# A two-layer graph network on one core: the first step's adjacency product of two pairs as one two-level product, and gate weights kept inside a matrix that has become free

## The chip, the core and the metric

The kernel runs on one core of a Trainium2 chip. The metric is device time in microseconds, lower is better. A run of the kernel before takes 1511.48 us (median of three, 1511.04 to 1511.8). Engines: PE (matmul) with its weight loads PEld, DVE (vector), ACT (activations), POOL (GpSimd), and SP, whose queue issues every DMA here. Everything is float32.

## What is computed

`x` is 32 batches of 512 nodes by 128 channels; `adj` is one 512 x 512 matrix, the same for all.

```python
# layer 0, K = 3, both adjacency matrices are adj
x_all = [x, adj x, adj^2 x, adj^3 x, adj x, adj^2 x, adj^3 x]
x = layernorm(x + einsum('bnik,iok->bno', x_all, weight_1))
# layer 1, five steps from h = x
m_in = m_out = adj @ h
av = concat(m_in, m_out)
u3 = h @ u3_w.T + u3_b
z  = sigmoid(av @ w3_w.T + w3_b + u3)
r  = sigmoid(av @ w4_w.T + w4_b + u3)
hv = tanh(av @ w5_w.T + w5_b + (r * h) @ u5_w.T + u5_b)
h  = (1 - z) * h + z * hv
# after the steps
x = layernorm(x + h)
```

Since `m_in` and `m_out` are equal, the two halves of w3, w4 and w5 are added once, to 128 x 128 matrices.

## The kernel before

**Work.** Batches go in 16 pairs. Each pair passes layer 0 (`layer0`), then five steps (`pair`, the loop over `s`), then the residual and the norm. A step of a pair is: the product adj h of both batches, a product with u3 for each batch, and `gates` for each batch (products with w4, w3, w5 of m, with u5 of r h; sigmoids and a tanh on ACT; sums on DVE; the update of h on POOL, L925). Then h is turned from channels-by-nodes to nodes-by-channels for the next step's product, by a DVE transpose in blocks of 32 and two DMA legs through DRAM (`turn`: four puts and a fetch), or, for the last steps of pairs 14 and 15 (`ON_PE`), by PE transposes.

**Products in seven terms.** A 2 x 2 block product is made from seven block products instead of eight, with sums of blocks formed beforehand. `seven` holds the pattern: seven PE terms into three PSUM banks, where four results are copied out by ACT and three added by DVE. `pair_product` uses it on one level for two batches: seven terms of two matmuls of 256 columns (128 columns each of left operand), with four POOL sums of 128 x 256 in front. The sums of adj's blocks lie in `T`. `quad_product` uses it on two levels for four batches: an upper product of seven, each of which is again a product of seven quarter blocks. Four of the upper terms run together (the A half, left sums in `SA`, results in `PA`), then three (the B half, `SB`, results in `M`), and five DVE sums join them (L672). The second-level sums of adj's blocks lie in `TT`. It is 49 matmuls of 128 columns. Before the change, `quad_product` serves layer 0 from pair 2 on, with pairs 2 and 3, 4 and 5, and so on; the steps use `pair_product`.

**Order.** Nothing is ordered by the hardware's own luck: `Plan` is a list scheduler that runs when the kernel is built. Each operation has an engine, a length, its predecessors, the buffers that it takes and gives back, and a key. Whenever an engine is free, it gets the ready operation with the lowest key whose buffers are free. The order in which operations come out is each engine's instruction order on the chip. Keys come from `KEYS` (one start per pair), plus 30 and `LONG` = 19 per step. Buffers are counted in `slots`: eight PSUM banks, so many tiles of each name, and two counts without memory, `two` (products in the making) and `inside` (pairs between entry and end). The sums that form `TT` are planned right after `T`; the summed gate weights w3s, w4s, w5s have tiles of their own.

**h0.** The input of layer 1 is kept for the residual. Except for the last three pairs it is written to DRAM after step 0's product has read it (hd<-h), and fetched back for the end.

**Gates.** `mm(dst, w, src, first, last)` is one matmul with 512 moving columns: the weights are stationary, m (128 channels x 512 nodes) moves.

Of the kernel before, what the change touches and what calls it, by code (L numbers as in the profile page):

```python
# [9 lines left out]
F32 = mybir.dt.float32  # L10
AF = mybir.ActivationFunctionType
ALU = mybir.AluOpType
PSUM = bass.MemoryType.PSUM

P = 128
NK = 4
N = NK * P
H = NK // 2
HN = N // 2
R = 32  # L20
NR = P // R
STEPS = 5
ON_PE = {14: 2, 15: 2}
KEYS = [8.0, 22.0, 60.0, 88.0, 108.0, 144.0, 174.0, 188.0, 210.0, 244.0, 274.0, 310.0, 338.0, 368.0, 384.0, 396.0]
LONG = 19.0
KEPT = 3
FIRST = 2
SINGLE = 2
EPS = 1e-5
# [95 lines left out]
def gnn_resnorm_kernel(  # L125
# [17 lines left out]
    nc = tc.nc  # L143
    NP = x.shape[0] // 2

    const = ctx.enter_context(tc.tile_pool(name="const", bufs=1))
    work = ctx.enter_context(tc.tile_pool(name="work", bufs=1))
    small = ctx.enter_context(tc.tile_pool(name="small", bufs=16))
    psum = ctx.enter_context(tc.tile_pool(name="psum", bufs=1, space=PSUM))
    dram = ctx.enter_context(tc.tile_pool(name="dram", bufs=1, space=bass.MemoryType.DRAM))  # L150

    def tiles(tag, n, shape=(P, N), pool=work):
        return [pool.tile(list(shape), F32, tag=f"{tag}_{i}", name=f"{tag}_{i}") for i in range(n)]

    slots = dict(
        bank=tiles("bank", 8, pool=psum),
        d=tiles("d", 6, (NR, R, NR, P), dram),
        hd=tiles("hd", 6, (P, 2, NK, P), dram),
        xg=tiles("xg", 2, (P, 2, NK, P)),
        xT=tiles("xT", 3),  # L160
        M=tiles("M", 1, (P, 4, N)),
        SA=tiles("SA", 1, (P, 25, P)),
        SB=tiles("SB", 1, (P, 15, P)),
        UY=tiles("UY", 2, (P, 4, N)),
        h0=tiles("h0", 4, (P, 2, NK, P)),
        hT=tiles("hT", 8),
        X=tiles("X", 3),
        uT=tiles("uT", 6),
        rh=tiles("rh", 2),
        z=tiles("z", 3),  # L170
        m=tiles("m", 5),
        S=tiles("S", 2, (P, 7, H, P)),
        v=tiles("v", 4),
        two=[None] * 3,
        inside=[None] * 14,
    )
    plan = Plan(slots)
# [12 lines left out]
    T = const.tile([P, 4, H, HN], F32, tag="T", name="T")  # L190
    TT = const.tile([P, 7, 4, P], F32, tag="TT", name="TT")
    make_identity(nc, ident)
# [35 lines left out]

    TT_sums = []
    for i, n, of in (  # L230
        (0, 4, lambda k, c: T[:, :, k, c]),
        (4, 2, lambda k, c: at.rearrange("p (o k) c -> p o k c", o=2)[:, :, k, c]),
        (6, 1, lambda k, c: at[:, H + k : H + k + 1, HN + c.start : HN + c.stop]),
    ):
        lo, hi = slice(0, P), slice(P, HN)
        b11, b12, b21, b22 = of(0, lo), of(0, hi), of(1, lo), of(1, hi)
        t = lambda j, i=i, n=n: TT[:, i : i + n, j, :]

        def emit(b11=b11, b12=b12, b21=b21, b22=b22, t=t):
            for j, (a, b) in enumerate(((b12, b11), (b22, t(0)), (b22, b12), (b21, t(1)))):  # L240
                nc.vector.tensor_tensor(t(j), a, b, ALU.subtract)  # L241

        TT_sums.append(plan("DVE", (2.8, 1.7, 1.12)[i // 3] if i else 2.8, emit, after=T_sums, key=22.0))

# [13 lines left out]
    w0_ready = plan("DVE", 2.3, layer0_weights, after=[w0_in], give=[("UY", "w0")], key=-40.0)  # L260


    ready = []

    def gate_weight(src, name):
        halves = lambda: plan[name][:, : 2 * P].rearrange("p (h o) -> p h o", h=2)
        w = const.tile([P, P], F32, tag=name, name=name)
        emit = lambda: nc.sync.dma_start(halves(), src.rearrange("(h c) o -> c h o", c=P))
        got = plan("SP", 0.45, emit, take=[("z", name)], key=-60.0, late=6.5)
        emit = lambda: nc.vector.tensor_tensor(w, halves()[:, 0, :], halves()[:, 1, :], ALU.add)  # L270
        ready.append(plan("DVE", 0.28, emit, after=[got], give=[("z", name)], key=-30.0))
        return w

    def plain(src, name):
        t = const.tile(list(src.shape), F32, tag=name, name=name)
        ready.append(plan("SP", 0.45, lambda: nc.sync.dma_start(t, src), key=-55.0, late=5.0))
        return t

    w3s, w4s, w5s = (gate_weight(s, n) for s, n in ((w3, "w3s"), (w4, "w4s"), (w5, "w5s")))
    u3s, u5s = plain(u3, "u3s"), plain(u5, "u5s")  # L280
    b3s, b4s, b5s = plain(b3, "b3s"), plain(b4, "b4s"), plain(b5, "b5s")
    ub3s, ub5s = plain(ub3, "ub3s"), plain(ub5, "ub5s")
    hv_b = const.tile([P, 1], F32, tag="hv_b", name="hv_b")
    hv_ready = plan("DVE", 0.1, lambda: nc.vector.tensor_tensor(hv_b, b5s, ub5s, ALU.add), after=ready, key=-30.0)
    weights = ready + [hv_ready]

# [131 lines left out]
    an_of = lambda km: plan[f"an{km // H}"].rearrange("p b k c -> p (b k c)").rearrange("p (k n) -> p k n", k=H)  # L418
    an_ready = []
    for km in range(NK):  # L420
        emit = lambda km=km: transposes(plan[f"ba{km}"], lambda k: at[:, k, chunk(km)])
        take = [("bank", f"ba{km}")] + ([("h0", f"an{km // H}")] if km % H == 0 else [])
        tr = plan("PE", 0.44, emit, after=at_in, take=take, key=20.0)
        emit = lambda km=km: nc.scalar.copy(an_of(km)[:, km % H], plan[f"ba{km}"])
        an_ready.append(plan("ACT", 0.59, emit, after=[tr], give=[("bank", f"ba{km}")], key=20.0))
# [49 lines left out]
    for i, (a, b, op) in enumerate(  # L475
        (
            (A21, A22, ALU.add),
            (at2S[:, 0], A11, ALU.subtract),
            (A11, A21, ALU.subtract),
            (A12, at2S[:, 1], ALU.subtract),  # L480
        )
    ):
        emit = lambda i=i, a=a, b=b, op=op: nc.vector.tensor_tensor(at2S[:, i], a, b, op)
        A2_sums.append(plan("DVE", 0.69, emit, after=squared + A2_sums[-2:], key=21.0))

    half_bank = lambda bank: bank[:, :HN]
# [65 lines left out]
    def quad_product(X_of, name, after, key):  # L552
# [48 lines left out]
        def right(block, sums):  # L601

            quarters = {0: (0, 0), 1: (1, 0), 6: (1, 1)}

            def R_of(i):
                if i in quarters:
                    k, c = quarters[i]
                    return block[:, k, c * P : (c + 1) * P]
                return TT[:, sums, {2: 1, 3: 0, 4: 2, 5: 3}[i]]

            return R_of
# [268 lines left out]

    def gates(name, m, h, after, u_done, quick, key):

# [5 lines left out]
        mm = lambda dst, w, src, first, last: nc.tensor.matmul(  # L888
            plan[dst], lhsT=w, rhs=plan[src], start=first, stop=last
        )  # L890
        take = [("bank", pr), ("rh", rh), ("z", z)]
        p = plan("PE", 0.86, lambda: mm(pr, w4s, m, True, True), after=after + weights + [u_done], take=take, key=key)
        emit = lambda: nc.vector.scalar_tensor_tensor(plan[pr], plan[pr], b4s, plan[uT], ALU.add, ALU.add)  # L893
# [4 lines left out]

        p2 = plan("PE", 0.86, lambda: mm(pz, w3s, m, True, True), after=[p], take=[("bank", pz)], key=key + 0.5)
        emit = lambda: nc.vector.scalar_tensor_tensor(plan[pz], plan[pz], b3s, plan[uT], ALU.add, ALU.add)  # L900
# [3 lines left out]

        emit = lambda: mm(ph, w5s, m, True, False)
        p3 = plan("PE", 0.86, emit, after=[p2], take=[("bank", ph)], give=[("m", m)], key=key + 0.7)
        emit = lambda: mm(ph, u5s, rh, False, True)
# [20 lines left out]
    def finish(q, b, name, h, parts, h0_of, after, key, done):  # L928
# [25 lines left out]
        done.append(plan("SP", 0.36, emit, after=over, key=key + 10, late=2.0))  # L954

    def pair(q, key0):

        entered = plan("-", 0.0, lambda: None, take=[("inside", f"in{q}")], key=key0)
        after, h_done = layer0(q, key0, [entered])
        h0_of = lambda b: plan[f"h0{q}"][:, b]  # L960
        h = [f"hT{q}_{b}" for b in range(2)]
        X_of, turned = h0_of, False
        for s in range(STEPS):
# [4 lines left out]
            for b in range(2):  # L968
# [7 lines left out]
                u_done.append(plan("ACT", 0.69, emit, after=[p], give=[("bank", bn)], key=key + 5))  # L976
            slots = [("S", f"S{name}")] + [("m", f"m{name}_{b}") for b in range(2)]
            S_of = lambda i, name=name: plan[f"S{name}"][:, i]
            dst = lambda i, j, name=name: plan[f"m{name}_{i}"][:, j * HN : (j + 1) * HN]
            got, read = pair_product(X_of, turned, name, dst, S_of, slots, after, key)  # L980
            if s == 0 and q < NP - KEPT:
# [21 lines left out]
            for b in range(2):  # L1003
                nm = f"{name}_{b}"
                Xb = f"X{nm}"
                quick = last and not by_dma
                d = gates(nm, f"m{nm}", h[b], got[b], u_done[b], quick, key + 10)
                if quick:
# [29 lines left out]
                stored = plan("SP", 0.36, emit, after=over, key=key + 17, late=2.0)  # L1038
                done.append(stored)
            if last:  # L1040
                plan("-", 0.0, lambda: None, after=done, give=[("h0", f"h0{q}")], key=key)
                plan("-", 0.0, lambda: None, after=h_done[0] + h_done[1], give=[("inside", f"in{q}")], key=key)
# [59 lines left out]
```

## Time and profile before

| | |
|---|---|
| median of three runs | 1511.48 us |
| profiled execution | 1511.12 us |
| its span, first to last instruction | 1509.3 us |
| last PE record ends | 1500.7 us after the start |
| PE records, weight loads | 6590, 6590 |
| DMA, share of 16 engines | 34.3% |

The profile is one execution. The page has the busy time of each engine, 40 slices of the span, the chain of work that ended last and the costliest groups. "x320" is a count of records; a float32 matmul leaves two records, a PE transpose one. The shapes of PE groups give weights (128*128) and output (128x256). Groups on the other engines that matter here, with busy us, mean ns and idle time before them:

```profile
L925 POOL TENSOR_TENSOR hT<-z,hT 128x512 f32<-128x512 f32 x156 | 198.3, 1276 | 256.4 <-DVE z L923 246.6
L372 ACT COPY m<-bank 128x256 f32<-128x256 f32 x320 | 119.2, 372 | 286.8 <-PE bank L511 284.9
L376 DVE TENSOR_TENSOR m<-bank,m 128x256 f32<-128x256 f32 x240 | 100.7, 420 | 120.4 <-PE bank L511 86.4
```

L511 is the matmul of `pair_product`, L615 that of `quad_product`, L749 and L811 are layer 0's products with its weights and with adj squared, L888 the gate products, L970 the product with u3, L936 the residual sums on PE in the last pairs.

### The profile page before, as it was taken

How to read it: one execution, taken by the hardware profiler on the slowest of the kernel's cores; microseconds unless marked ns; L12 is line 12 of the kernel's file. 1: busy time of each engine (PE TensorE's matmuls, PEld its weight loads, DVE VectorE, ACT ScalarE, POOL GpSimd, SP SyncE). 2: the span in 40 equal slices, each digit the busy share in tenths (PEclk: the TensorE clock that was granted, in tenths of full speed). 3: DMA queues.
4: the chain of work that ended last, by engine and by line, in shares of the span. 5: the costliest groups of instructions: out<-in, count | busy, mean ns of one | idle time of the engine just before them, and what ended most of it. 6: DMA issues, size and time to landing. Idle time of an engine off the chain costs nothing.

```text
span 1509.3 us, 21208 instructions
## 1 busy us (share of the span) xinstructions
PE 1493.1 (99%) x6590; PEld 1044.1 (69%) x6590; DVE 1021.8 (68%) x2123; ACT 749.1 (50%) x1582; POOL 844.3 (56%) x1201
## 2 busy tenths in 40 slices
PE   8999999999999999999999999999999999999997
PEld 7877667667676767676767667677776776665665
DVE  6566676775776667665775766776578665767665
ACT  3354544455445545554454554554545544555454
POOL 4846754665645856663663665656665643544442
PEclk9999999999999999999999999999999999999999
DMA  3223333243333434233333443443343323433310
GB/s 96 71 57 98 104 86 112 81 123 98 98 113 89 123 81 142 82 109 90 98 98 99 117 116 88 112 133 92 97 109 100 80 70 80 108 101 82 84 36 35
DMA packets 165889, 142.91 MB, mean 95 GB/s; under 512 B 18961, under 2 KB 127505, under 8 KB 165777
## 3 DMA queue, kind: packets, MB, share of 16 engines
q1 hardware_dynamic: 165776, 141.57, 34.3%
q8 instruction: 52, 0.85, 0.3%
q14 instruction: 61, 0.49, 0.1%
HBM read 71.76 MB, written 69.73 MB: 94 GB/s over the span
## 4 chain that ended last, share of the span: by engine, by line
PE 97%; DMA 1%; DVE 1%; SPq 0%; POOL 0%; ACT 0%; issue 0%; POOLq 0%; DVEq 0%
PE bank L888 36%; PE bank L511 32%; PE bank L970 9%; PE bank L811 7%; PE bank L749 6%; PE bank L615 5%; PE bank L936 1%; PE bank L447 1%; DMA z<-in_w 0%; PE bank L290 0%; DMA X<-d 0%; DVE TT L241 0%; DMA xg<-in_x 0%; POOL S L498 0%; ACT h L318 0%
## 5 line engine op out<-in xcount | busy, mean ns | idle before, releaser
L925 POOL TENSOR_TENSOR hT<-z,hT 128x512 f32<-128x512 f32 x156 | 198.3, 1276 | 256.4 <-DVE z L923 246.6
L511 PE MATMUL bank<-T,S 128*128 128x256 f32 x1232 | 307.1, 379 | 0.2
L511 PEld LDWEIGHTS bank<-T,S 128*128 128x128 f32 x1232 | 228.4, 190 | 75.3 <-ACT m L372 32.0
L372 ACT COPY m<-bank 128x256 f32<-128x256 f32 x320 | 119.2, 372 | 286.8 <-PE bank L511 284.9
L511 PE MATMUL bank<-at,S 128*128 128x256 f32 x824 | 211.3, 379 | 0.0
L511 PEld LDWEIGHTS bank<-at,S 128*128 128x128 f32 x824 | 153.4, 190 | 57.4 <-issue 36.7
L376 DVE TENSOR_TENSOR m<-bank,m 128x256 f32<-128x256 f32 x240 | 100.7, 420 | 120.4 <-PE bank L511 86.4
L921 DVE TENSOR_TENSOR bank<-bank,hT 128x512 f32<-128x512 f32 x156 | 108.3, 695 | 107.6 <-ACT bank L909 106.8
L888 PE MATMUL bank<-m,w4s 128*128 128x512 f32 x320 | 159.7, 592 | 0.0
L888 PE MATMUL bank<-m,w3s 128*128 128x512 f32 x320 | 157.5, 592 | 0.0
L888 PE MATMUL bank<-rh,u5s 128*128 128x512 f32 x320 | 156.9, 592 | 0.0
L970 PE MATMUL bank<-hT,u3s 128*128 128x512 f32 x320 | 156.5, 592 | 0.0
L893 DVE SCALAR_TENSOR_TENSOR bank<-bank,b4s,uT 128x512 f32<-128x512 f32 x160 | 119.9, 752 | 52.8 <-PE bank L888 48.5
L888 PE MATMUL bank<-m,w5s 128*128 128x512 f32 x320 | 155.0, 592 | 0.0
L909 ACT ACTIVATE bank<-bank,hv_b 128x512 f32<-128x512 f32 x160 | 105.5, 662 | 89.4 <-PE bank L888 87.9
L895 ACT ACTIVATE bank<-bank 128x512 f32<-128x512 f32 x160 | 93.2, 583 | 102.8 <-DVE bank L893 102.6
L975 ACT ACTIVATE uT<-bank,ub3s 128x512 f32<-128x512 f32 x160 | 109.7, 687 | 58.9 <-PE bank L970 57.7
L902 ACT ACTIVATE z<-bank 128x512 f32<-128x512 f32 x160 | 94.2, 595 | 64.4 <-DVE bank L900 60.2
L900 DVE SCALAR_TENSOR_TENSOR bank<-bank,b3s,uT 128x512 f32<-128x512 f32 x160 | 118.6, 751 | 11.1 <-PE bank L888 9.8
L347 DVE STREAM_TRANSPOSE v<-hT 128x512 f32<-128x512 f32 x152 | 105.7, 701 | 12.7 <-POOL hT L925 11.4
L896 DVE TENSOR_TENSOR rh<-bank,hT 128x512 f32<-128x512 f32 x160 | 107.5, 680 | 8.3 <-ACT bank L895 7.8
L376 DVE TENSOR_TENSOR UY<-bank,UY 128x256 f32<-128x256 f32 (+1 forms) x117 | 54.4, 467 | 82.0 <-PE bank L749 36.2
(163 smaller groups left out, 2500.8 us busy)
## 6 DMA issues: line engine op xcount, KB each, us to landing
d<-v SPq DMA_DIRECT2D x832, 64.0 KB, 1.8
X<-d SPq DMA_DIRECT2D x152, 256.0 KB, 2.8
v<-d SPq DMA_DIRECT2D x56, 256.0 KB, 2.8
xg<-in_x SPq DMA_DIRECT2D x32, 256.0 KB, 3.0
out<-h SPq DMA_DIRECT2D x32, 256.0 KB, 2.0
hd<-h SPq DMA_DIRECT2D x13, 512.0 KB, 3.9
h<-hd SPq DMA_DIRECT2D x13, 512.0 KB, 3.9
at<-in_adjT SPq DMA_DIRECT2D x4, 256.0 KB, 4.7
```

What stands on the lines that cost most here:

```text
L347: blocks = lambda: nc.vector.transpose(plan[f"v{name}"], src_of())
L372: return "ACT", COPY[cols], lambda src: nc.scalar.copy(dst(i, j), src)
L376: return "DVE", ADD[cols], lambda src: nc.vector.tensor_tensor(dst(i, j), src, dst(i, j), ALU.add)
L511: nc.tensor.matmul(dst, lhsT=left[:, k, :], rhs=right[:, k, :], start=(first and k == 0), stop=(last and k == H - 1), skip_group_check=True,)
L888: mm = lambda dst, w, src, first, last: nc.tensor.matmul(plan[dst], lhsT=w, rhs=plan[src], start=first, stop=last)
L893: emit = lambda: nc.vector.scalar_tensor_tensor(plan[pr], plan[pr], b4s, plan[uT], ALU.add, ALU.add)
L896: emit = lambda: nc.vector.tensor_tensor(plan[rh], plan[pr], plan[h], ALU.mult)
L900: emit = lambda: nc.vector.scalar_tensor_tensor(plan[pz], plan[pz], b3s, plan[uT], ALU.add, ALU.add)
L921: emit = lambda: nc.vector.tensor_tensor(plan[ph], plan[ph], plan[h], ALU.subtract)
L925: emit = lambda: nc.gpsimd.tensor_tensor(plan[h], plan[z], plan[h], ALU.add)
L970: emit = lambda bn=bn, hb=h[b]: nc.tensor.matmul(plan[bn], lhsT=u3s, rhs=plan[hb], start=True, stop=True)
L975: emit = lambda bn=bn, uT=uT: nc.scalar.activation(plan[uT], plan[bn], AF.Identity, bias=ub3s)
```

## The change

Step 0 of the pairs from 2 up to `JOINT` (16, so all) uses `quad_product` as well: the even pair's call makes the product for both pairs, as layer 0 does. For that, `pair` now plans layer 0 of both pairs of a quad before the first one's steps. The result lies in an `M` tile in which a batch's 512 columns are two pieces of 256, not next to each other; so `gates` takes a function `m(j)` and makes each product with w4, w3 and w5 as two matmuls of 256 columns. It does so in every step, not in step 0 alone.

The second `M` tile needs room. The gate weights move into the block B12 of `at`, which has no reader after the sums `T` and the four transposes that lead to adj squared; the seventh group of `TT` moves into block A21 of `at2`, so its sums come after those of `at2S`. `small` has 12 instead of 16 buffers, `uT` 4 instead of 6, `hT` 9 instead of 8, `two` is 8 instead of 3, `inside` 18 instead of 14. `KEYS` are new, and of pair 14 only the last step is turned on PE, not the last two.

```diff
-ON_PE = {14: 2, 15: 2}
-KEYS = [8.0, 22.0, 60.0, 88.0, 108.0, 144.0, 174.0, 188.0, 210.0, 244.0, 274.0, 310.0, 338.0, 368.0, 384.0, 396.0]
+ON_PE = {14: 1, 15: 2}
+KEYS = [10.0, 24.0, 68.0, 80.0, 96.0, 128.0, 162.0, 168.0, 188.0, 220.0, 232.0, 284.0, 304.0, 336.0, 354.0, 364.0]
+JOINT = 16
...
-        M=tiles("M", 1, (P, 4, N)),
+        M=tiles("M", 2, (P, 4, N)),
-        hT=tiles("hT", 8),
+        hT=tiles("hT", 9),
-        uT=tiles("uT", 6),
+        uT=tiles("uT", 4),
-        two=[None] * 3,
-        inside=[None] * 14,
+        two=[None] * 8,
+        inside=[None] * 18,
...
+    TT_of = lambda i, j: TT[:, i, j, :] if i < 6 else A21[:, j // H, (j % H) * P : (j % H + 1) * P]
...
-        w = const.tile([P, P], F32, tag=name, name=name)
+        w = spare(B12)
...
-        ready.append(plan("DVE", 0.28, emit, after=[got], give=[("z", name)], key=-30.0))
+        ready.append(plan("DVE", 0.28, emit, after=[got] + B12_read, give=[("z", name)], key=-30.0))
...
+        def from_m(dst, w, last):
+            for j in range(2):
+                nc.tensor.matmul(
+                    plan[dst][:, j * HN : (j + 1) * HN],
+                    lhsT=w,
+                    rhs=m(j),
+                    start=(j == 0),
+                    stop=last,
+                    skip_group_check=True,
+                )
...
-        p = plan("PE", 0.86, lambda: mm(pr, w4s, m, True, True), after=after + weights + [u_done], take=take, key=key)
+        p = plan("PE", 0.86, lambda: from_m(pr, w4s, True), after=after + weights + [u_done], take=take, key=key)
...
+        for i in range(q, q + 2 if q >= SINGLE and (q - SINGLE) % 2 == 0 else q + 1):
+            if i not in first:
+                entered = plan("-", 0.0, lambda: None, take=[("inside", f"in{i}")], key=KEYS[i])
+                first[i] = layer0(i, KEYS[i], [entered])
...
+            quad = s == 0 and SINGLE <= q < JOINT
+            Mn = f"Mh{q - i}"
+            if quad:
+                if i == 0:
+                    X_four = lambda b: plan[f"h0{q + b // 2}"][:, b % 2]
+                    steps0[q] = quad_product(X_four, f"h{q}", after + first[q + 1][0], key)
+                got, read = (o[2 * i : 2 * i + 2] for o in steps0[q - i])
+                m_of = lambda b, i=i, Mn=Mn: lambda j: plan[Mn][:, 2 * j + i, b * HN : (b + 1) * HN]
```

In the changed file the matmul of `quad_product` is L628, that of `pair_product` L524, the gate products are L909 (w4, w3, w5) and L903 (u5), and the product with u3 is L1004.

## What the change was predicted to do

> **What bounds the kernel now.** I read, in this order: the page's busy times and its slices, the chain of work that ended last, PE's own waits, the stretches of the span, and then single rows of the timeline for the pace of a matmul.
>
> ```profile
> PE 1493.1 (99%) x6590; PEld 1044.1 (69%) x6590; DVE 1021.8 (68%) x2123; ACT 749.1 (50%) x1582; POOL 844.3 (56%) x1201
> ...
> PEclk9999999999999999999999999999999999999999
> ...
> PE 97%; DMA 1%; DVE 1%; SPq 0%; POOL 0%; ACT 0%; issue 0%; POOLq 0%; DVEq 0%
> ```
>
> ```profile
> PE bank L290 <- DMA xg<-in_x: 4.5, 2, 3.6
> PE bank L749 <- DVE UY L376: 1.3, 1, 1.3
> PE bank L749 <- ACT UY L372: 0.9, 2, 0.5
> PE bank L290 <- ACT h L318: 0.4, 1, 0.4
> ```
>
> The second fence is all that PE waited for in the whole span (total us, times, longest). 97% of the chain is PE, its clock is full, and its waits sum to 7.1 us. The stretches show where those are (columns: stretch, its length, then busy us and records of PE and PEld, DVE, ACT, POOL):
>
> ```profile
> 0.00:20.00 20.00, 15.29 (x76) 12.43 (x77) 11.60 (x26) 7.74 (x14) 7.70 (x13) 1.00 0.58 180
> 20.00:60.00 40.00, 37.23 (x247) 33.66 (x247) 22.11 (x54) 14.05 (x35) 25.30 (x37) 1.00 0.10 28
> 60.00:1480.00 1420.00, 1419.93 (x6155) 982.41 (x6154) 972.36 (x1994) 716.53 (x1510) 805.00 (x1139) 1.00 0.36 97
> 1480.00:1510.00 30.00, 20.68 (x117) 15.65 (x115) 15.73 (x50) 10.82 (x24) 6.26 (x14) 0.92 0.09 36
> ```
>
> From 60 to 1480 us PE is idle for 0.07 us. So the time is PE's work plus a fixed head and tail, and a change is worth what it takes off PE's work, less what idle time it puts into that dense stretch.
>
> The pace, from neighbouring starts in the timeline:
>
> ```profile
> 221.71 1.05 PE L615 MATMUL bank<-TT,SA 128*128 128x128 f32 x8
> 222.60 1.02 PE L970 MATMUL bank<-hT,u3s 128*128 128x512 f32 x2
> 223.46 1.02 PE L888 MATMUL bank<-rh,u5s 128*128 128x512 f32 x2
> ...
> 702.47 1.89 PE L511 MATMUL bank<-T,S 128*128 128x256 f32 x8
> 704.20 1.02 PE L888 MATMUL bank<-m,w4s 128*128 128x512 f32 x2
> ```
>
> Each f32 matmul is two records (320 records for 160 calls of L970). 0.89/8 = 0.111 us a record at 128 columns, 1.73/8 = 0.216 at 256, 0.86/2 = 0.43 at 512. The means over all start-to-start distances of the trace are 111.6 (L615), 216.0 and 429.4 ns; a matmul is thus 0.2232, 0.4320 and 0.8588 us. The printed means (275, 379, 592 ns) overlap and must not be summed.
>
> **The Trainium skill.** "Perfetto Trace Analysis", section Identifying the Most-Contended Engine, says that matmul busy time is a bad measure because matmuls are pipelined; the trace agrees (592 ns printed, 429 ns of pace), so I count paces. "FP8 and Floating Point Precision" says true FP32 takes four passes, and "TensorE: Matmul & The Clock Gate", section Back-to-back issue gap, gives about N/2.4 + 2.5 ns for a pass; here two passes a record at 512 columns would be 432 ns by that, and 429 is measured: columns pay, and cutting a matmul in two costs a few ns only. "VectorE: DVE Perf Modes", section Two Vector instructions with no wait between them, mentions a second SBUF read interface shared with GpSimd. The trace fits: L672, which adds two SBUF tensors on DVE, takes 645 ns at its shortest and 1590 at its longest, and means 856 to 989 in its three groups.
>
> **The change, part by part.**
>
> 1. Step 0 of pairs 2 to 15. Two pair products are 2 x 14 matmuls of 256 columns, 28 x 0.4320 = 12.10 us. The joint product is 49 matmuls of 128 columns, 49 x 0.2232 = 10.94 us. 1.16 us less, in seven quads: -8.1 us. All of it is on PE, so all on the path.
>
> 2. Gate products. w4, w3 and w5 against m are now two matmuls of 256 columns instead of one of 512, for all 160 calls: 480 x (2 x 0.4320 - 0.8588) = +2.5 us. Twice the weight loads, but L511 already runs loads of this shape behind 216 ns of pace. Bounds +1 and +3.
>
> 3. One step of pair 14 goes from PE transposes to DMA: 8 transposes of about 0.11 us leave PE, -0.9 us. In their place stand two DVE block transposes, 8 puts of 64 KB and 2 fetches on SP's queue, and a few copies. SP issues about 0.43 us per DMA, 1140 of them, so a third of its time. The distances of part 6 show that pair's next product nowhere late; cost 0, and some 3 us once if PE had nothing else in that gap, since the two legs land 1.8 and 2.8 us after their issue.
>
> PE's work: -8.1 + 2.5 - 0.9 = -6.5 us. A count over both built programs gives the same: 128 columns 1287 to 1630, 256 columns 1176 to 1940, 512 columns 800 to 320, transposes 64 to 56.
>
> 4. Other engines. A quad on POOL is 16.5 us of adds by the rows of before (six halves at 0.73, four quarters at 0.46, four triples at 1.00, then eleven adds of SB, 6.3 us) in place of eight at 0.73: +10.6, seven times +75 us, so POOL goes from 56 to about 61%. DVE: 3 x 0.68 + 4 x 0.548 + 3 x 0.551 + five sums of L672 (4.5 us) in place of six of 0.42: +7.9, seven times +55, 68 to 72%. ACT loses about 4 us. None becomes the bound; each is hidden under PE as long as other pairs' matmuls stand in PE's queue.
>
> 5. Gate weights in at's spare block. Their three DVE sums now wait for the four transposes that read the block. Those run until 12.1 us in before, and the sums at 14.1: covered by 2 us. The seventh group of TT moves behind at2's sums; nothing needs it before the first quad, near 60 us. Cost 0; if the cover were gone, about 1 us once. In the head the built order also lets pair 1's first products in ahead of the row that waited 1.3 us for UY at 25.6, so -1 to +1; I take 0.
>
> 6. Idle time in the dense stretch. Here the order itself tells something. I laid PE's queue at the paces above and, for each matmul, summed the ACT, DVE, POOL and DMA steps back to the last matmul that they depend on, without queueing. In before, no matmul after 60 us is late by more than 0.02 us. In after, four are. About 170 us in, the third, fifth and sixth terms of one pair product stand directly behind each other, with nothing between; each needs ACT's copy of the one before (about 0.2 + 0.37 + 0.1), late by 0.69 us twice. Near 287 and 1057 us a second-level product has only 0.44 us of other work in front of it where 0.9 is wanted: 0.47 us each. Sum +2.3 us. It is a lower bound, since queueing is left out; an upper one is one such pair of holes per quad, 7 x 1.4 = 10 us. The load by stretches of 10 us on DVE and POOL has the same peaks in both orders (12 us on either), and in before these caused no stall, so I take 2.3.
>
> The tail: the last rows are the same two batches' gates, sums and norm, so the 8.6 us after the last matmul stay.
>
> Sum: 1511.12 us of the profiled execution (span 1509.3 and 1.8 around it) - 6.5 + 2.3 = 1506.9. The median of the three runs is 0.36 higher, 1511.48: 1507.3. No change here means within 0.2%, 3.0 us, that is 1508.5 to 1514.5.
>
> **Rivals.**
>
> A. The holes of part 6 don't show, since before has shown no stall at all in the dense stretch and the head may gain: 1511.5 - 6.5 = 1505.0. Against: a product that stands behind its own copy has nothing to overlap with.
>
> B. My forecast, 1507.3.
>
> C. The gain is mostly given back. Pairs now walk in twos, and both must have left layer 0 before either's step 0; at 150 to 185 us PE's queue is already short of independent work. With 3.5 to 9 us of idle time the change can't be told from none: about 1510.5.
>
> D. Slower. Place: POOL's queue at the seven joint products. A state update (L925, 1.28 us) stands behind adds of up to 1.3 us each, and the two-operand sums of DVE lengthen while POOL reads, as L672 shows. The update releases the block transpose, four puts and a fetch, and only then the next product. If each quad leaves PE without work for over 1.36 us (9.5/7), the sum is past +3; at 2 us it is 14 - 6.5 = +7.5, 1519. For it: 14 instead of 7 such bursts. Against: the seven of before stall PE for nothing, and POOL is idle 39% of the time.
>
> That the change does not do what it says, a 128-column matmul costing more than its pace, is excluded by L615 and L811, which run so in 1582 records.
>
> **How the numbers follow.** A 0.28, B 0.38, C 0.19, D 0.15. Faster is A and B, 0.66; within 0.2% is C; slower is D. The range from 1504.0 to 1513.0 takes in A's sum with 1 us of gain in the head, and C to most of its width; it leaves out D and A's last edge.
>
> **What would show it.** Records at L628 (the joint products) 1372 instead of 686, at paces of 112 ns; gate records of 256 columns at 216 ns; PE's busy time near 1487. Waits of PE beyond 60 us of 2 to 3 us, at the products near 170, 287 and 1057 us. Wrong, if the gate records pace above 218 ns, if PE waits for POOL or DMA inside the dense stretch by more than 4 us, or if the head grows by over 1 us.

## The result and the profile after

The changed kernel takes 1515.15 us (median of 11 runs, 1513.97 to 1521.59), the kernel before 1511.63 beside it (11 runs, 1511.04 to 1512.41). The ratio is 1.0027 with a 95% interval of 1.0018 to 1.0037: 2.7 to 5.6 us slower. The profiled execution is 1515.1 us with a span of 1513.3, against 1511.12 and 1509.3 before: +4.0.

The page of the kernel after, busy times and the shares of the chain of work:

```profile
PE 1492.5 (99%) x7836; PEld 1227.9 (81%) x7836; DVE 1077.3 (71%) x2188; ACT 745.7 (49%) x1554; POOL 923.0 (61%) x1321
...
PE 93%; DVE 2%; POOL 2%; DMA 1%; SPq 1%; issue 1%; ACT 0%; POOLq 0%; DVEq 0%; ACTq 0%
```

PE is at 99% as it was, and that says nothing. The chain says more: 97% of it was PE, now 93%, with DVE and POOL at 2% each. The stretches of the span, columns as before:

```profile
0.00:20.00 20.00, 14.80 (x75) 12.19 (x76) 11.94 (x24) 7.37 (x13) 9.49 (x15) 1.00 0.60 180
20.00:60.00 40.00, 37.84 (x252) 34.32 (x251) 22.65 (x58) 14.89 (x36) 24.95 (x37) 1.00 0.10 28
60.00:1480.00 1420.00, 1415.36 (x7372) 1160.76 (x7372) 1024.88 (x2055) 709.68 (x1476) 880.72 (x1256) 1.00 0.35 97
```

The head is as it was (52.64 us of PE in the first 60, 52.52 before). The dense stretch is not: PE is idle for 4.64 us between 60 and 1480 us, where it was 0.07. And PE's waits over the whole span (total us, times, longest):

```profile
PE bank L249 <- DMA xg<-in_x: 5.0, 3, 3.5
PE bank L628 <- DVE M L332: 2.3, 6, 0.6
PE bank L524 <- ACT m L331: 0.9, 2, 0.5
...
PE bank L628 <- ACT UY L331: 0.5, 2, 0.2
PE bank L524 <- ACT S L504: 0.3, 1, 0.3
```

The first row is the head. The second is new, the largest in the dense stretch, and was not forecast: a matmul of a joint product waits for DVE, six times.

**How much time is lost.** These views hide part of it. The modelled end of a matmul lies some 0.16 us after the next one could have started, so a hole shows that much too short, and one under 0.16 us not at all (a matmul of 128 columns is printed as 0.275 us and paces at 0.112). I therefore took, for each pair of neighbouring PE starts, the distance less the pace of the first (0.1116, 0.216, 0.4294 us by columns, 0.110 for a transpose). The sum is 7.6 us before, all of it in the first 100 us, and 18.0 after: 7.1 in the first 100 us and 10.9 between 100 and 1400. So the lost time grew by 10.4 us, and PE's work fell by 10.4 - 4.0 = 6.4. That PE's busy time is 1492.5, where the prediction had 1487, is the same thing: it covers 10.9 - 4.6 = 6.3 us of the holes.

Where the 10.9 are: 2.0 at the four places of part 6 (177.6, 179.2, 297.6 and 1074.5 us), 3.3 in the six waits of L628 for L332 (200.5, 549.8, 567.7, 754.4, 984.2, 1146.3 us), and 5.6 in smaller ones, such as pair products that wait for ACT's copy or for POOL's sums. Of these 5.6, about 1.0 is a second delay of 0.10 us that follows just behind each of the ten waits named.

The longest of the six, as the chain of waits has it between 745 and 757 us (start, length, what):

```profile
747.39 1.80 PE bank L628 x16
749.19 0.02 issue
749.22 0.70 DVE UY L335
...
750.01 0.95 DVE UY L685
750.96 1.14 DVE M L685
752.10 0.67 DVE bank L920
752.77 1.09 DVE M L685
753.86 0.48 DVE M L332
754.34 0.04 issue
754.38 0.94 PE bank L628 x6
```

L628 ends the A half. DVE adds its last result (L335), then takes the joining sums (L685, formerly L672) as they become ready; a gate sum (L920) comes between; and behind them stands L332, the first addition of the B half, which PE's next term needs. PE runs out of other work at 753.6. Four more of the six have two or three sums of L685 in front of L332 in the same way. At 984.2 us it is the statistics of a norm (L260, L261) that stand there, and no sum of L685. The timeline of DVE and POOL around 750 us shows why the sums are long:

```profile
749.68 0.73 POOL L511 TENSOR_TENSOR S<-UY 128x256 f32<-128x256 f32 x1
...
750.01 0.95 DVE L685 TENSOR_TENSOR UY<-UY 128x512 f32<-128x512 f32 x1
...
750.37 1.18 POOL L511 TENSOR_TENSOR S<-UY,S 128x256 f32<-128x256 f32 x1
...
750.89 1.21 DVE L685 TENSOR_TENSOR M<-UY 128x512 f32<-128x512 f32 x1
...
752.68 1.18 DVE L685 TENSOR_TENSOR M<-M,UY 128x512 f32<-128x512 f32 x1
...
753.27 1.18 POOL L511 TENSOR_TENSOR S<-xT,M 128x256 f32<-128x256 f32 x1
```

A sum of L685 that has no POOL addition beside it takes 0.68 us (16 of them, 0.651 to 0.692). One with POOL beside it for over 0.6 of its length takes 1.08 on average (43, among them one of 4.19; 1.00 without it). POOL's own adds of 128x256 go from 0.73 to 1.18 where they meet one. The groups of the kernel after:

```profile
L685 DVE TENSOR_TENSOR M<-M,UY 128x512 f32<-128x512 f32 x42 | 39.8, 971 | 0.3
L332 DVE TENSOR_TENSOR M<-bank,UY 128x384 f32<-128x384 f32 x56 | 30.7, 549 | 10.3 <-PE bank L628 9.7
L685 DVE TENSOR_TENSOR M<-UY 128x512 f32<-128x512 f32 x14 | 14.9, 1067 | 0.0
L685 DVE TENSOR_TENSOR UY<-UY 128x512 f32<-128x512 f32 x14 | 12.6, 901 | 0.7
```

And two of the kernel before:

```profile
L672 DVE TENSOR_TENSOR M<-M,UY 128x512 f32<-128x512 f32 x21 | 17.4, 856 | 0.2
L373 DVE TENSOR_TENSOR M<-bank,UY 128x384 f32<-128x384 f32 x28 | 15.4, 548 | 6.8 <-PE bank L615 6.8
```

L332, which reads one operand from PSUM, means 549 ns, before (as L373) 548. Of these groups only the sums of two SBUF tensors lengthen. The Trainium skill, "SBUF — State Buffer", says in the section Who interferes with whom that a DVE instruction with two SBUF inputs contends with a GpSimd instruction that reads SBUF, and in the section SBUF: two separate sides that the one which starts first has the shared ports for its whole length while the other fully blocks. The trace agrees on which instructions lengthen (L685, and not L332), and it shows either engine's as the longer one: the sum that starts at 750.01 takes 0.95 instead of 0.68 us, the POOL add at 750.37 takes 1.18 instead of 0.73.

### The profile page after: what moved, and what is told of

Same layout as the page of the kernel before. It is cut to its first block, busy times and chain, and to the rows that moved or that the text cites. A ratio compares the mean times of both kernels' runs of the same rounds, so it can differ in the third digit from the quotient of the medians.

```text
span 1513.3 us, 23806 instructions
## 1 busy us (share of the span) xinstructions
PE 1492.5 (99%) x7836; PEld 1227.9 (81%) x7836; DVE 1077.3 (71%) x2188; ACT 745.7 (49%) x1554; POOL 923.0 (61%) x1321
## 4 chain that ended last, share of the span: by engine, by line
PE 93%; DVE 2%; POOL 2%; DMA 1%; SPq 1%; issue 1%; ACT 0%; POOLq 0%; DVEq 0%; ACTq 0%
PE bank L909 27%; PE bank L524 25%; PE bank L1004 9%; PE bank L903 9%; PE bank L628 9%; PE bank L824 7%; PE bank L762 6%; PE bank L407 1%; PE bank L964 1%; DMA v<-d 1%; DVE M L685 1%; POOL S L511 0%; DMA z<-in_w 0%; POOL SB L511 0%; SPq L298 0%
## 5 line engine op out<-in xcount | busy, mean ns | idle before, releaser
L909 PE MATMUL bank<-m,at 128*128 128x256 f32 x1584 | 377.8, 379 | 0.1
L909 PEld LDWEIGHTS bank<-m,at 128*128 128x128 f32 x1584 | 293.1, 190 | 55.8 <-issue 19.9
L524 PE MATMUL bank<-T,S 128*128 128x256 f32 x1068 | 266.0, 380 | 1.1 <-ACT m L331 0.9
L524 PEld LDWEIGHTS bank<-T,S 128*128 128x128 f32 x1068 | 197.2, 190 | 47.4 <-ACT m L331 17.8
L331 ACT COPY m<-bank 128x256 f32<-128x256 f32 x264 | 98.3, 372 | 234.8 <-PE bank L524 232.9
L524 PE MATMUL bank<-at,S 128*128 128x256 f32 x776 | 199.7, 380 | 0.3 <-ACT S L504 0.3
L524 PEld LDWEIGHTS bank<-at,S 128*128 128x128 f32 x776 | 143.2, 190 | 38.1 <-issue 15.8
L1004 PE MATMUL bank<-hT,u3s 128*128 128x512 f32 x320 | 159.5, 593 | 0.0
L335 DVE TENSOR_TENSOR m<-bank,m 128x256 f32<-128x256 f32 x198 | 82.7, 418 | 106.8 <-PE bank L524 68.3
L903 PE MATMUL bank<-rh,u5s 128*128 128x512 f32 x320 | 158.4, 593 | 0.1
L920 DVE SCALAR_TENSOR_TENSOR bank<-bank,b4s,uT 128x512 f32<-128x512 f32 x160 | 119.5, 751 | 41.3 <-PE bank L909 39.1
L331 ACT COPY UY<-bank 128x256 f32<-128x256 f32 (+1 forms) x184 | 79.8, 436 | 106.0 <-PE bank L762 68.0
L335 DVE TENSOR_TENSOR UY<-bank,UY 128x256 f32<-128x256 f32 (+1 forms) x138 | 68.1, 496 | 62.5 <-PE bank L762 27.2
```

The source lines that it names most:

```text
L331: return "ACT", COPY[cols], lambda src: nc.scalar.copy(dst(i, j), src)
L335: return "DVE", ADD[cols], lambda src: nc.vector.tensor_tensor(dst(i, j), src, dst(i, j), ALU.add)
L524: nc.tensor.matmul(dst, lhsT=left[:, k, :], rhs=right[:, k, :], start=(first and k == 0), stop=(last and k == H - 1), skip_group_check=True,)
L903: mm = lambda dst, w, src, first, last: nc.tensor.matmul(plan[dst], lhsT=w, rhs=plan[src], start=first, stop=last, skip_group_check=True)
L909: nc.tensor.matmul(plan[dst][:, j * HN : (j + 1) * HN], lhsT=w, rhs=m(j), start=(j == 0), stop=last, skip_group_check=True,)
L1004: emit = lambda bn=bn, hb=h[b]: nc.tensor.matmul(plan[bn], lhsT=u3s, rhs=plan[hb], start=True, stop=True)
```

## Experiments

Differences are to the kernel after where not said otherwise; "lost" is time over the pace between 100 and 1400 us in the profiled execution (10.9 in the kernel after, nothing before). Only one execution of each kernel is profiled, and those of one kernel differ by 1 to 8 us in time, so a difference of 1 or 2 us lost means little. The ratios are to the kernel before.

**e1: the cut gate products alone.** The kernel before, its order untouched, with w4, w3 and w5 applied in two matmuls of 256 columns.

```diff
+        def cut(dst, wt, last):
+            for j in range(2):
+                c = slice(j * HN, (j + 1) * HN)
+                nc.tensor.matmul(plan[dst][:, c], lhsT=wt, rhs=plan[m][:, c], start=(j == 0), stop=last, skip_group_check=True)
...
-        p = plan("PE", 0.86, lambda: mm(pr, w4s, m, True, True), after=after + weights + [u_done], take=take, key=key)
+        p = plan("PE", 0.86, lambda: cut(pr, w4s, True), after=after + weights + [u_done], take=take, key=key)
```

> The kernel before with only the gate products cut into two matmuls of 256 columns; every engine keeps its order. The prediction's term 2 says +2.5 us against before (2 x 216.0 - 429.4 = 2.6 ns on each of 960 records), bounds +1 to +3. Rival: the cut itself lets PE stall or pace above 218 ns, which would be +5 us or more and would explain the whole slowdown.

Measured: 1513.98 us, ratio 1.0015 (1.0007 to 1.0022), so 1.1 to 3.3 us; the span grew by 2.2. Nothing was lost beyond the head. Its dense stretch:

```profile
60.00:1480.00 1420.00, 1420.00 (x7094) 1161.11 (x7093) 969.46 (x1991) 714.85 (x1506) 803.33 (x1138) 1.00 0.35 97
```

The second term (+2.5) is right, and 960 more weight loads put no hole into it.

**e2: whole gate products where m is one piece.** The order of the kernel after, with the 2 us of the cut taken back.

```diff
         def from_m(dst, w, last):
+            if m_tile:
+                nc.tensor.matmul(plan[dst], lhsT=w, rhs=plan[m_tile[0][1]], start=True, stop=last, skip_group_check=True)
+                return
```

> The changed kernel, but a step whose m lies in one piece (all but step 0 of pairs 2 to 15) takes its gate products with one matmul of 512 columns again: 396 of 480 products, same order on every engine. By the pace -396 x 5.2 ns = -2.1 us against the changed kernel, about 1513.1. The idle time of PE stays near 18 us. Rival, the cut hides more than its pace: over 4 us less.

Measured: 1517.7 us (5 runs, 1513.97 to 1518.14), ratio 1.0034 (1.0022 to 1.0047). A miss: no gain. The lost time rose from 10.9 to 14.2, by more than the 2 us that PE's work fell by. Shorter matmuls in this order only brought PE earlier to the next wait: where the kernel after loses time, PE is not what sets the pace.

**e3: thin joining sums.** Four of the five sums of L685, all but `v`, on 128 of their 512 columns (the rest of their result is left out). This goes for the joint products of layer 0 too, which share the code.

```diff
-        def dve(d, a, b, after):
-            emit = lambda: nc.vector.tensor_tensor(d(), a(), b(), ALU.add)
+        def dve(d, a, b, after, c=P):
+            emit = lambda: nc.vector.tensor_tensor(d()[:, :c], a()[:, :c], b()[:, :c], ALU.add)
...
-        v = dve(M_of(3), PA_of(1), PA_of(2), ends + [own])
+        v = dve(M_of(3), PA_of(1), PA_of(2), ends + [own], N)
```

> The changed kernel with four of the five DVE sums that join a joint product's halves on 128 of their 512 columns (these sums are left out for three quarters of their columns); same order on every engine. Theory 1, these sums stand in DVE's queue ahead of what PE waits for and are lengthened by POOL: PE's idle time inside 60 to 1480 us falls from 11 to about 4 us, the waits of L628 for DVE M go, -5 to -7 us. Rival, PE lacks independent work because pairs walk in twos: under 1 us.

Measured: 1510.42 us (13 runs), ratio 0.9993 (0.9984 to 1.0001); 4.7 us under the kernel after, the span 5.5. Lost: 5.7. The waits for L332 are gone from PE's waits, and the chain of the same stretch as above is PE alone:

```profile
749.17 2.01 PE bank L628 x18
751.17 1.73 PE bank L524 x8
752.90 0.67 PE bank L628 x6
```

**e4: thin POOL adds.** All of POOL's adds for the joint products on 32 of each 128 columns (the others are left out); L685 is whole.

```diff
+    nc.vector.memset(slots["SA"][0], 0.0)
+    nc.vector.memset(slots["SB"][0], 0.0)
...
-    def add(us, dst, a, b, op, after, key):
-        emit = lambda: nc.gpsimd.tensor_tensor(dst(), a(), b(), op)
+    def add(us, dst, a, b, op, after, key, thin=False):
+        few = lambda t: (t[:, :32] if len(t.shape) == 2 else t[:, :, :32]) if thin else t
+        emit = lambda: nc.gpsimd.tensor_tensor(few(dst()), few(a()), few(b()), op)
```

> The changed kernel with POOL's adds of the joint products on 32 of each 128 columns (these sums are left out for three quarters of their columns); same order, POOL's busy time falls by over 100 us. Theory 2, POOL's queue delays updates and left sums: the losses at products that wait for S or for m go as well, -6 us or more, more than the thin DVE sums give. Theory 1: only the lengthening of the DVE sums goes (from about 0.97 to 0.69), -2 to -4 us. Rival, too little independent work: under 1 us.

Measured: 1510.59 us (13 runs), ratio 0.9992 (0.9984 to 1.0); 4.6 us under the kernel after, although the two memsets cost 1.6 us in the head. That lies between the 2 to 4 us of theory 1 and the 6 or more of theory 2. Lost: 5.7, as in e3; of the six waits for L332 (here L334) one is left, of 0.2 us, and the products that wait for ACT's copies of m stay as they were, against theory 2. The sums, now L688 and untouched by the edit, are shorter (971, 1067 and 901 ns in the kernel after):

```profile
L688 DVE TENSOR_TENSOR M<-M,UY 128x512 f32<-128x512 f32 x42 | 33.6, 825 | 0.3
L688 DVE TENSOR_TENSOR M<-UY 128x512 f32<-128x512 f32 x14 | 12.7, 910 | 0.0
L688 DVE TENSOR_TENSOR UY<-UY 128x512 f32<-128x512 f32 x14 | 11.4, 814 | 0.7
```

Either engine's share taken away brings about the same gain and removes the waits for L332. That, and that the two gains do not add up in e5, is what one shared cause does; two separate ones would not.

**e5: both thin.** The edits of e3 and e4 together.

> The changed kernel, same order, with the four thin DVE sums and the thin POOL adds together (both sets of sums are left out for three quarters of their columns). If each alone removed the same losses, DVE sums that overlap POOL's adds, both together bring little more than either: 1509 to 1511, and about 5 us of idle time remain that the order itself holds. If they are two separate causes their gains add: about 1506.

Measured: 1509.55 us (21 runs), ratio 0.9987 (0.998 to 0.9993). 5.6 us under the kernel after and not the sum of 4.7 and 4.6. Lost: 4.7; the four holes of part 6 stay. So 5 to 6 of the 10.9 us hang on DVE's sums and POOL's adds, and about 5 remain without them, in the order itself.

**f1, f7: the joint product in a new order.** Gates as in e2; every length that the scheduler uses set to the measured one (L685 0.98 instead of 0.69, the terms of 16 records 0.893 instead of 0.88, and so on), and new `KEYS` searched for with these. f7 is the same kernel again.

```diff
-            return plan("DVE", 0.69, emit, after=after, key=key)
+            return plan("DVE", 0.98, emit, after=after, key=key)
...
-        s0 = add(0.73, F(0), X21, X22, ALU.add, both, key)
+        s0 = add(0.75, F(0), X21, X22, ALU.add, both, key)
```

> The joint product in step 0 as in the changed kernel, gates whole where m is in one piece, the joining sums entered in the plan at 0.98 us and the other lengths at their measured values (joint terms 0.893 and 0.67, sums on POOL 0.75, 1.01, 0.46), and new KEYS found for that. If the loss came from an order made with lengths that the chip doesn't keep, PE's idle time inside 60 to 1480 us falls from 11 to about 5 us, and with 2.1 us less for whole gates the time is 1505 to 1507, 5 to 7 below before. Rival, the joint product's extra work on DVE and POOL costs PE the same in any order: idle time stays at 9 or more, time 1511 or above.

> The kernel of f1 once more, beside f5 and f6 on the same chip, because f1's one profile was of its slowest execution. Both theories: 1509 to 1511. Expected of its profile: PE idle between 60 and 1480 us about 3 to 4 us instead of 7, without the waits at, S <- ACT of 3 us.

Measured: f1 1510.19 us (13 runs, ratio 0.9996, 0.9988 to 1.0004), f7 1511.86 (13 runs, ratio 1.0, 0.9992 to 1.0009). A miss: 1505 to 1507 was expected of f1, and f7's profile was to show 3 to 4 us of idle time, where it has 5.3. The kernel is 3 to 5 us faster than the one after, some 2 of them for the whole gates, and not to be told from the kernel before. That one kernel gave medians 1.7 us apart shows how far a difference can be trusted here. f7 loses 9.1 us and f1, profiled in its slowest execution (1514.18), 10.8: hardly less than the kernel after. The waits for L332 have shrunk to one of 0.34 us in the starts; others have come in their place, for ACT's copies, one of them of a layer's result that had only just landed by DMA. Planning with the mean length did not remove the idle time.

**f2: the kernel before in a new order.** The control: measured lengths and a new search, no joint product in step 0.

> Control: the kernel before with the same measured lengths and new KEYS found with as long a search. It has little idle time to give (0.35 us beyond the first 100 us), so 1510 to 1512, at most 2 us below before. If it gains as much as the other replanned kernel, the gain there is of the search and not of the joint product.

Measured: 1513.83 us (16 runs), ratio 1.0015 (1.0008 to 1.0023). That is above the 1510 to 1512 expected. The new search is no gain by itself; f1 doesn't owe its time to it.

**f3: pairs in twos without the joint product.** The kernel after with measured lengths, whole gates and new keys, its buffers and the place of its gate weights kept, but step 0 is two single products again, which wait for layer 0 of both pairs of their quad.

```diff
-            quad = s == 0 and SINGLE <= q < JOINT
+            quad = False
+            if s == 0 and i == 0 and SINGLE <= q < JOINT:
+                after = [a + [o for n in first[q + 1][0] for o in n] for a in after]
```

> Step 0 as two single products, as before, but waiting until both pairs of a quad have left layer 0; gates whole, measured lengths, new KEYS found for it. If walking in twos is what starves PE, its idle time inside 60 to 1480 us is 5 us or more and the time 1516 or above. If the joint product's extra sums are, there is next to no idle time (under 2.5 us) and the time is that of the replanned kernel before, 1512 to 1514.5.

Measured: 1515.25 us (8 runs), ratio 1.0029 (1.0019 to 1.004), 1.4 over f2, with intervals that touch; lost 3.6, f2 1.2. This lies between what the two theories expected. Walking in twos (rival C's reason) may cost 1 to 2 us, more by the ends of the intervals. With the smaller `uT` and the other new buffer counts, which f3 has too, it doesn't carry the 10.9 us.

**f4: the joint product planned with short sums.** As f1, but the scheduler is told 0.69 us for L685, as in the kernel after, with keys of its own.

> The replanned joint kernel, but the joining sums entered at 0.69 us as in the changed kernel, with KEYS found by as long a search. If it matters that the plan knows the sums' real length, the waits of L628 for DVE M come back (2 us or more) and the time is 1512 to 1515. If any order with few planned holes does, it equals the other replanned joint kernel, 1509 to 1511.

Measured: 1524.62 us (4 runs), ratio 1.0087 (1.0074 to 1.0101), worse than either theory had it. Lost: 23.0 (in the slowest of the four executions), nearly all that it has beyond f7 at the three waits of one row:

```profile
PE bank L628 <- DVE UY L335: 8.4, 3, 3.4
```

By the starts of the matmuls these are 9.8 us, and 13.9 with the smaller holes that follow within 4 us. Before each of the three stands a sum of L685 of 4.45, 4.75 or 4.92 us. f1 and f4 are one order each, so this doesn't show that the planned length alone makes the difference.

**f5, f6: the joining sums on POOL.** As f1, with new keys. f5 moves the first two of the five, f6 all five. The lines shown are from f6, where the last two sums change in the same way.

```diff
+        pool = lambda d, a, b, after: add(1.28, d, a, b, ALU.add, after, key)
...
-        u = dve(PA_of(3), PA_of(3), PA_of(0), ends)
-        v = dve(M_of(3), PA_of(1), PA_of(2), ends + [own])
-        e22 = dve(M_of(3), M_of(3), PA_of(3), [u, v])
+        u = pool(PA_of(3), PA_of(3), PA_of(0), ends)
+        v = pool(M_of(3), PA_of(1), PA_of(2), ends + [own])
+        e22 = pool(M_of(3), M_of(3), PA_of(3), [u, v])
```

> As f1 (joint products, whole gates where m is one piece, lengths as measured, keys found anew), but the first two of the five joining sums of each joint product, u and v, stand on POOL at 1.28 us instead of DVE at 0.98. No part of the computation is left out. Theory (the loss is DVE's: joining sums in its queue, lengthened by POOL's two-operand adds): with two of five sums off DVE, and never beside another two-operand add on POOL, PE's waits for DVE's additions of banks shrink below 1 us; the kernel's own plan is 1.1 us longer than f1's, so 1509 to 1511. Rival (POOL's queue is the scarce one, at 62% busy): state updates L925 wait behind the moved sums, the waits return as PE for DVE M or DMA X, 1512 or more.

> As f5, with all five joining sums of each joint product on POOL at 1.28 us, none on DVE. No part of the computation is left out. Theory: no long DVE sum is left to stand in front of the B half's first additions or to be held by POOL, so the idle time of PE between 60 and 1480 us falls to what the order itself holds, 2 to 3 us, and the time to 1507.5 to 1510. Rival: POOL, at about 64% busy, now carries 6.4 us in one run after each B half, and the updates behind it are late: 1512 or more.

Measured: f5 1512.38 us (13 runs, ratio 1.0006, 0.9998 to 1.0014), f6 1509.0 (21 runs, ratio 0.9983, 0.9977 to 0.999).

f5 is a miss, and loses 12.3 us (in an execution of 1514.66). In time it falls to the rival, but not by the rival's waits. Its first row beyond the head is "PE bank L628 <- DVE UY L335: 4.4, 3, 1.8", and the timeline of DVE and POOL shows what it is:

```profile
1077.58 1.15 POOL L511 TENSOR_TENSOR SB<-h,SA 128x256 f32<-128x256 f32 x2
1077.72 4.43 DVE L685 TENSOR_TENSOR M<-M,UY 128x512 f32<-128x512 f32 x1
1078.67 0.88 POOL L511 TENSOR_TENSOR SB<-SB,h 128x128 f32<-128x128 f32 x2
1079.50 0.88 POOL L511 TENSOR_TENSOR SB<-h,SB 128x128 f32<-128x128 f32 x2
1080.33 1.28 POOL L511 TENSOR_TENSOR SB<-SB,SA 128x512 f32<-128x512 f32 x1
```

One DVE sum is held for as long as POOL adds without a break, and ends 0.54 us after POOL's run does (1082.15 against 1081.61). That the two sums moved to POOL let the rest start in the middle of its run is likely, but not shown: in f4 sums were held in the same way with none moved.

f6 has no sum left on DVE that POOL could hold. Its sums, and POOL's adds that read h0:

```profile
L511 POOL TENSOR_TENSOR M<-M,UY 128x512 f32<-128x512 f32 x42 | 52.7, 1271 | 13.2 <-DVE M L335 13.0
...
L511 POOL TENSOR_TENSOR SA<-h,h 128x256 f32<-128x256 f32 x14 | 10.2, 729 | 0.0
```

1.27 us each, where DVE took 0.68 alone and 0.97 in the mix. POOL's adds SA<-h,h, which stood beside them, fell to 729 ns from 832 in the kernel after:

```profile
L511 POOL TENSOR_TENSOR SA<-h,h 128x256 f32<-128x256 f32 x14 | 11.6, 832 | 0.0
```

PE waits for no L332 or L335 of a joint product. POOL is at 66%. The time is the only one of a kernel with nothing left out that lies clearly below that of before, by 1.5 to 3.5 us. It is also below f7's, measured beside it, but with other keys, so what the place of the sums gave isn't separated from the order. The idle time was mis-said: 5.1 us in the dense stretch (in an execution of 1511.54 us, 2.5 over the median), not 2 to 3, in waits that the new order brought:

```profile
PE bank L524 <- ACT m L331: 2.3, 2, 1.8
PE bank L524 <- ACT S L504: 2.2, 3, 1.4
```

Lost: 8.6. So even in f6 most of what PE's work fell by, 8 to 9 us, is given back.

## Why the prediction was wrong

**Parts 1 to 3, PE's work: right.** Forecast -6.5, measured -6.4. L628 has 1372 records at a median pace of 112 ns, the gate records a mean of 216.5. e1 measures part 2 by itself: +2.2 in span. The formula that the prediction took from the Trainium skill, "TensorE: Matmul & The Clock Gate", section Back-to-back issue gap, is given there for an isolated matmul; the measured paces, and e1, carry the term.

**Part 4, the other engines: right as shares, wrong as a comfort.** POOL at 61% and DVE at 71% came as said (71 for 72). "None becomes the bound" holds for the mean and not for the places where PE waits.

**Part 5, the head: right.** 7.1 us lost in the first 100 us against 7.6.

**Part 6, idle time in the dense stretch: the step that failed.** The four holes came where they were put, 2.0 us for 2.3. The term itself was 10.9 us (10.4 with the head's gain), not 2.3. It had been called a lower bound, because queueing was left out, and was then taken as the value, since "the load by stretches of 10 us on DVE and POOL has the same peaks in both orders (12 us on either), and in before these caused no stall, so I take 2.3". Equal peaks of load don't tell who stands behind whom. What was left out is two things.

The first is queueing in the order as written. The scheduler is part of the kernel and keeps a clock, with lengths from its code. On that clock, PE is idle between 60 and 1470 us for 1.3 us in the kernel before and 9.5 after. The list has my four holes, and places near 404 to 411, 982 and 1134 to 1137 where the trace, some us later, loses time as well. It also has some that the trace does not show, such as 1.7 us near 789, so that the two totals are close is in part chance: the places that both have make up about half of the 9.5. For f1, f4, f5 and f6 the same clock has 5.2, 6.1, 4.2 and 5.4 us, and the traces 10.8, 23.0, 12.3 and 8.6. A layout with queues would thus have warned before any run, but it would not have given the number. What the order loses without the contention is better read from e5: 4.7 us, 2.0 of them at the four holes.

The second is that the lengths aren't fixed. The scheduler, and my sum, give L685 0.68 or 0.69 us; beside POOL it takes 1.08. On the scheduler's clock the hole of 754 us doesn't exist. The three sums ahead of L332 took 0.95 + 1.14 + 1.09 = 3.18 us there; at 0.68 they are 1.14 us shorter, and the hole is 0.77. e4, which takes POOL's side of it away, gains 4.6 us in time; e3, which takes away the sums' own length too, 4.7, and both together 5.6. In lost time both together take away 6.2 of the 8.6 us by which part 6 was too low.

**The rivals.** The time fell between C (1510.5) and D (1519). D's reason was half right: "the two-operand sums of DVE lengthen while POOL reads, as L672 shows" is the mechanism, and the lost time over all places, 10.4/7 = 1.5 us a quad, is past the 1.36 us from which D was to decide. Its place was wrong. It was to be POOL's queue, with late updates at L925; it is DVE's queue, in five of the six long waits with L332 behind L685. What spoke against D, that "the seven of before stall PE for nothing", was taken for a property of the burst. But in before the same sums are long as well, 856 to 989 ns on average, and PE is idle for 0.07 us. It seems to have been a matter of what PE had to do meanwhile; no run tests that by itself. C's reason, the pairs in twos, is some 1 to 2 us by f3.

**Open.** Why f2's order, with its small losses, has a median over that of before. Why runs of one and the same kernel spread over 3 to 8 us in all other orders (1513.97 to 1521.59 in the kernel after, 1506.76 to 1512.1 in f6), where 41 runs of before stay within 2.7. And the 4.7 us that e5 keeps are seen place by place, but no run removed them, so that they are in the order is argued.

## What to carry to other kernels

Where an engine is busy without a gap, the saving on it is the easy term. Lay out the new order with every queue, in the order in which the instructions stand, and with lengths that hold when the neighbour engine is busy; equal load is no evidence. A length measured alone is not one to plan with where DVE adds two SBUF tensors beside POOL: here 0.68 us became anything up to 4.92. Planning with the mean of 0.98 was not enough (f1, f7); with all these additions on POOL the kernel was clearly faster than before (f6). Each of these is a single order, so this is a thing to try and not a rule. Once PE has holes, a microsecond less of its work isn't a microsecond less of time (e2).

## What the runs showed of the hardware

- A DVE sum of two SBUF tensors of 128x512 takes 0.68 us alone and 1.08 on average beside POOL, but it can also be shut out for the whole of an unbroken run of POOL adds. Seven such sums of 3.5 to 4.9 us were followed (one in the kernel after, which cost PE nothing, and three each in f4 and f5). Every one started 0.1 to 0.3 us after an instruction of POOL had and ended 0.55 us after POOL's run did, and POOL's instructions in that run kept within 0.05 us of their usual lengths. The second section cited above says that the second to start blocks while the first runs; that it can lose to six to eight instructions in a row is more than it says. Why other sums, as at 750 us, got in between two adds isn't settled.
- 960 more records on PE with as many more weight loads cost 2.2 us (e1), 2.3 ns each.
- A wait that reads 0.60 us in the view of waits was 0.77 in the starts of the matmuls. Over the dense stretch PE's busy time leaves 4.64 us idle, where the starts have 10.9.
